# Selective scans by halves of the channels: two states with elementwise products, two with products on TensorE, per slice

## The chip, the cores and the metric

The kernel runs on one core of a Trainium2 chip. A core has a matrix engine (TensorE, PE in the profile), a vector engine (VectorE, DVE), an activation engine (ScalarE, ACT), a general engine (GpSimd, POOL) and a queue engine (SyncE, SP) that here only starts transfers. Each engine executes its own instructions in order, and engines wait for one another by semaphores. The metric is the device time of one execution in microseconds (us). The kernel before takes 34339.38 us (median of three runs, 34338.59 to 34341.42).

## The reference, cut to what matters

The program is a chain of four layers on an image of 256 x 256 positions with 128 channels. Layer 0 is an attention along rows, layer 1 a selective scan in four directions, layer 2 mixes Fourier modes, layer 3 convolves by FFT. Only layer 1 is concerned. For each of the directions `k`, with 256 inner channels `d` and 16 states `n`, it computes along the 65536 positions `t`

```
delta = softplus(dts + dt_bias)
dA    = exp(delta[t, d] * A[d, n])
h     = dA * h + (delta[t, d] * x[t, d]) * B[t, n]      # the state, one recurrence per (d, n)
y[t, d] = sum_n h[d, n] * C[t, n]
```

`B` and `C` depend on position and state and are the same for all channels. `delta * x` (called `du` in the kernel) depends on position and channel and is the same for all states. The results of the four directions are added.

## The kernel before, in words

`scan_stream` computes layer 1's recurrences. It cuts each direction into 128 chunks of `CH` = 512 positions, so there are N = 512 chunks in all, one after another. Channels lie on the 128 partitions, in two halves `dh`. In a chunk there are `NG` = 8 groups of `G` = 4 states: even groups belong to half 0, odd ones to half 1. A group goes through these steps:

- `b_product` (L769): `db = B * du` for four states, 128 x 2048 elements. B comes from DRAM, broadcast to all partitions (`load_b`, L692). Of each eight groups, those in `on_pool` (three) run on POOL, the other five on DVE, which reads `du` out of PSUM.
- `scans` (L771 to L808): two scans of 1024 elements, each two states of 512 in a row. Two exponentials on ACT (L787) write `dA` into one of two PSUM tiles `das`. At the joint of the two states `dA` has to be zero, so that the second state starts anew. The position `mid` is set to zero by a memset on DVE (L783), but only at the very first group and once more where the direction of time turns; after that no one writes `mid`. A small activation (L791) adds the second state's carried value to `db` at the joint. Then DVE scans (L802).
- `keep_state` (L813): ACT copies the last column of the four states.
- `c_product` (L817): POOL multiplies `h` by C (`load_c`, L698).
- `sums` (L827): 16 transposing matmuls of 128 x 128 with the identity add the four states up in a PSUM bank per half, `ys`.

Once per half and chunk `delta` and `du` are made: `dt` (a matmul into PSUM, L704), `soft_abs`, `soft_exp`, `soft_sum` (softplus on ACT and PE, L716 to L729), `delta_copy` (L739), `delta_x` (DVE, L747), and for one half `du_copy` (ACT, L758). `xproj` (L672) and `xd_copy` (L684) make B and C of a later chunk. `y_turn`, `y_back` and `y_out` (L824 to L880) turn the summed result back and take it out of PSUM; `y_start` (L844) begins a new sum.

The order on every engine is written out by hand: the loop at L906 calls the steps in the order in which each engine has them, under a manual schedule. The tile framework adds the semaphore waits. It derives them from the order of the calls and from the tiles that each touches, and orders two engines on one PSUM tile whichever of its elements they touch. All transfers of the stage are issued by SP, in order.

Of the kernel before, what the change touches and what calls it, by code (L numbers as in the profile page):

```python
# [576 lines left out]
def scan_stream(c, xc2, y, w):  # L577
# [8 lines left out]
    G, BL, NG = 4, 1024, 8  # L586
    R = y[1].shape[3]
    NW = BL // S
    on_pool = (2, 4, 6)
    b_order = {0: (3,), 1: (4,), 2: (5,), 3: (6, 7), 4: (8,), 6: (10,)}  # L590
# [5 lines left out]
    with ExitStack() as a:  # L596
        st = a.enter_context(tc.tile_pool(name="l1b_st", bufs=1))
        io = a.enter_context(tc.tile_pool(name="l1b_io", bufs=2))
        bcp = a.enter_context(tc.tile_pool(name="l1b_bc", bufs=3))
        wk = a.enter_context(tc.tile_pool(name="l1b_wk", bufs=2))  # L600
        dram = a.enter_context(tc.tile_pool(name="l1b_dr", bufs=4, space=DRAM))
        ps1 = a.enter_context(tc.tile_pool(name="l1b_p1", bufs=1, space=PSUM))
        states = [st.tile([P, 2, 16], F32, name=f"l1b_state{k}") for k in range(4)]

        xds = [st.tile([64, CH], F32, name=f"l1b_xd{i}") for i in range(3)]
        for s in states:
            nc.vector.memset(s, 0.0)
        for xd in xds:
            nc.vector.memset(xd[32:64], 1.0)
        ys = [ps1.tile([P, CH], F32, name=f"l1b_y{dh}") for dh in range(2)]  # L610
        das = [ps1.tile([P, 2, CH], F32, name=f"l1b_da{i}") for i in range(2)]


        mm = ps1.tile([P, CH], F32, name="l1b_mm")
        du1 = ps1.tile([P, CH], F32, name="l1b_du")
        blocks, bcs, bbs, ccs, soft, dls, dbs, hs, hcs, yts = ({} for _ in range(10))
# [49 lines left out]

        def xproj(ch):
            if ch >= N:
                return
            k = chunks[ch][0]  # L670
            for dh in range(2):
                nc.tensor.matmul(  # L672
                    du1[:40],
                    w["xproj"][:, dh, k, :],
                    in_block(blocks[ch][0], ch, dh),
                    start=dh == 0,
                    stop=dh == 1,
                )

        def xd_copy(ch):  # L680
            if ch >= N:
                return
            xd = xds[ch % 3]
            nc.scalar.copy(xd[:40], du1[:40])  # L684
            bc = bcs[ch] = dram.tile([32, CH], F32, name="l1b_bc")
            nc.sync.dma_start(bc, xd[8:40])

        def load_b(m):
            if m < 4 * N:
                n0 = m % 4 * G  # L690
                bb = bbs[m] = bcp.tile([P, G, CH], F32, name="l1b_bb")
                nc.sync.dma_start(bb, bcs[m // 4][n0 : n0 + G][None].to_broadcast([P, G, CH]))  # L692

        def load_c(m):
            if m < 4 * N:
                n0 = 16 + m % 4 * G
                cc = ccs[m] = bcp.tile([P, G, CH], F32, name="l1b_cc")
                nc.sync.dma_start(cc, bcs[m // 4][n0 : n0 + G][None].to_broadcast([P, G, CH]))  # L698


        def dt(ch, dh):
            if ch >= N:
                return
            nc.tensor.matmul(  # L704
                mm,
# [6 lines left out]
        def soft_abs(ch):  # L712
            if ch >= N:
                return
            soft[ch] = wk.tile([P, CH], F32, name="l1b_tail", bufs=1)
            nc.scalar.activation(soft[ch], mm, AF.Abs)  # L716
            nc.scalar.activation(mm, mm, AF.Relu)

        def soft_exp(ch):
            if ch >= N:  # L720
                return
            tail = soft[ch]
# [3 lines left out]
        def soft_sum(ch):  # L726
            if ch >= N:
                return
            nc.tensor.matmul(  # L729
                mm, c.ident, soft.pop(ch), start=False, stop=True, skip_group_check=True  # L730
            )

        def delta_copy(ch, dh):

            if ch >= N:
                return
            k = chunks[ch][0]
            dl = dls[ch, dh] = wk.tile([P, CH], F32, name=f"l1b_dl{dh}")
            nc.scalar.copy(dl, mm)  # L739
            af = dls[ch, dh, "first"] = wk.tile([P, 16], F32, name=f"l1b_af{dh}")  # L740
            t0 = CH - 1 if k >= 2 else 0
            nc.scalar.activation(af, w["A"][:, k, dh], AF.Exp, scale=dl[:, t0 : t0 + 1])

        def delta_x(ch, dh):
            if ch >= N:
                return
            nc.vector.tensor_tensor(  # L747
                like_block(du1 if dh else mm, ch),
                like_block(mm, ch),
                in_block(blocks[ch][0], ch, dh),  # L750
                ALU.mult,
            )

        def du_copy(ch):
            if ch >= N:
                return
            dls[ch, "du"] = wk.tile([P, CH], F32, name="l1b_dus")
            nc.scalar.copy(dls[ch, "du"], mm)  # L758

        def b_product(g):  # L760
            ch, j = divmod(g, NG)
            if ch >= N:
                return
            db = dbs[g] = wk.tile([P, G, CH], F32, name="l1b_db", bufs=5)
            if j in on_pool:
                eng, du = nc.gpsimd, dls[ch, "du"]
            else:
                eng, du = nc.vector, du1 if j % 2 else mm
            eng.tensor_tensor(db, bbs[g // 2], du[:, None, :].to_broadcast([P, G, CH]), ALU.mult)  # L769

        def scans(g, extras):  # L771
            ch, j = divmod(g, NG)
            k, dh, n0, rev = chunks[ch][0], j % 2, j // 2 * G, chunks[ch][0] >= 2
            db = dbs.pop(g).rearrange("p g t -> p (g t)")
            h = hs[g] = wk.tile([P, G, CH], F32, name="l1b_h", bufs=3)
            hf = h.rearrange("p g t -> p (g t)")
            dl, af = dls[ch, dh], dls[ch, dh, "first"]
            mid = CH - 1 if rev else CH
            for i in range(2):
                one, two = n0 + 2 * i + rev, n0 + 2 * i + 1 - rev  # L780
                da = das[i].rearrange("p g t -> p (g t)")
                if g == 0 or ch == N // 2 and j == 0:
                    nc.vector.memset(da[:, mid : mid + 1], 0.0)  # L783
                for n in (one, two):
                    o = n % 2 * CH
                    lo, hi = (0, CH) if n == one else (0, CH - 1) if rev else (1, CH)
                    nc.scalar.activation(  # L787
                        da[:, o + lo : o + hi], dl[:, lo:hi], AF.Exp, scale=w["A"][:, k, dh, n : n + 1]
                    )
                first = db[:, 2 * i * CH + mid : 2 * i * CH + mid + 1]  # L790
                nc.scalar.activation(  # L791
                    first,
                    states[k][:, dh, two : two + 1],
                    AF.Identity,
                    scale=af[:, two : two + 1],
                    bias=first,
                )
                sl = slice(2 * i * CH, 2 * i * CH + 2 * CH)
                h_, a_, d_ = hf[:, sl], da, db[:, sl]
                if rev:  # L800
                    h_, a_, d_ = h_[:, ::-1], a_[:, ::-1], d_[:, ::-1]
                nc.vector.tensor_tensor_scan(  # L802
                    h_, a_, d_, states[k][:, dh, one : one + 1], ALU.mult, ALU.add
                )
                if i == 0 and g:
                    keep_state(g - 1)
                for extra in extras[i]:
                    extra()  # L808

        def keep_state(g):  # L810
            ch, j = divmod(g, NG)
            k, dh, n0 = chunks[ch][0], j % 2, j // 2 * G
            nc.scalar.copy(states[k][:, dh, n0 : n0 + G], hs[g][:, :, 0 if k >= 2 else CH - 1])  # L813

        def c_product(g):
            hc = hcs[g] = wk.tile([P, G, CH], F32, name="l1b_hc", bufs=3)
            nc.gpsimd.tensor_tensor(hc, hs[g], ccs[g // 2], ALU.mult)  # L817
            hs.pop(g - 1, None)

        def y_turn(ch, dh):  # L820
            if ch < 0:
                return
            yt = yts[dh] = wk.tile([P, CH], F32, name="l1b_yt", bufs=1)
            nc.scalar.copy(yt, ys[dh])  # L824

        def turned(to, b, part, start, stop):
            nc.tensor.matmul(  # L827
                to[:, bass.ts(b, P)],
                part,
                c.ident,  # L830
                start=start,
                stop=stop,
                is_transpose=True,
                skip_group_check=True,
            )

        def y_start(ch, dh):
            k = chunks[ch][0]
            xc, yo = blocks[ch]
            for b in range(CH // P):  # L840
                if k == 2:
                    turned(ys[dh], b, in_block(yo, ch, dh)[:, bass.ts(b, P)], b == 0, True)
                if k == 0:
                    nc.tensor.matmul(  # L844
                        ys[dh][:, bass.ts(b, P)],
# [7 lines left out]
        def sums(g):  # L853
            ch, j = divmod(g, NG)
            new = chunks[ch][0] % 2 == 1
            if j < 2 and not new:
                y_start(ch, j)
            hc = hcs.pop(g)
            for i in range(G):
                for b in range(CH // P):  # L860
                    turned(
                        ys[j % 2], b, hc[:, i, bass.ts(b, P)], new and j < 2 and i + b == 0, True
                    )

        def y_back(ch, dh):
            if ch < 0:
                return
            add = chunks[ch][0] == 3
# [927 lines left out]
```

## Time and profile before

| what | value |
|---|---|
| median of the runs | 34339.38 us |
| the profiled execution's own time | 34336.33 us |
| its span, first to last instruction | 34334.6 us |
| DVE busy | 31153.8 us (91%) |
| POOL busy | 27466.5 us (80%) |
| PE busy | 23728.7 us (69%) |
| ACT busy | 23345.7 us (68%) |
| the scans (L802): first start, last start | 3912.9 us, 29617.4 us |
| mean granted clock of TensorE | 0.804 |

The page of a profile has a row for each group of instructions: line, engine, operation, output and inputs by the program's names, shapes, count, then busy time, the mean duration of one in ns, and the idle time of the engine just before them with what ended most of it. The stage of the scans takes three quarters of the time, so a row's share of the whole understates its share of the stage.

### The profile page before, as it was taken

How to read it: one execution, taken by the hardware profiler on the slowest of the kernel's cores; microseconds unless marked ns; L12 is line 12 of the kernel's file. 1: busy time of each engine (PE TensorE's matmuls, PEld its weight loads, DVE VectorE, ACT ScalarE, POOL GpSimd, SP SyncE). 2: the span in 40 equal slices, each digit the busy share in tenths (PEclk: the TensorE clock that was granted, in tenths of full speed). 3: DMA queues.
4: the chain of work that ended last, by engine and by line, in shares of the span. 5: the costliest groups of instructions: out<-in, count | busy, mean ns of one | idle time of the engine just before them, and what ended most of it. 6: DMA issues, size and time to landing. Idle time of an engine off the chain costs nothing. (4 is left out here: it accounts for less than half of the span.)

```text
span 34334.6 us, 330861 instructions
## 1 busy us (share of the span) xinstructions
PE 23728.7 (69%) x108660; PEld 15714.0 (46%) x108660; DVE 31153.8 (91%) x23679; ACT 23345.7 (68%) x48143; POOL 27466.5 (80%) x6996
## 2 busy tenths in 40 slices
PE   7999766666666666666666666666666666799877
PEld 3554444444444444444444444444444444434444
DVE  6668999999999999999999999999999999873699
ACT  3667777777777777777777777777777777532477
POOL 2446899999999999999999999999999999720000
PEclk9999877777777777777777777777887787899999
DMA  3113455555555555555555555555555555675111
GB/s 141 45 45 123 185 190 189 191 190 190 189 191 189 189 190 190 190 189 191 195 201 199 201 200 200 199 202 200 200 202 200 201 199 201 209 233 160 68 35 33
DMA packets 2076823, 5952.61 MB, mean 173 GB/s; under 512 B 115207, under 2 KB 1379608, under 8 KB 1499222
## 3 DMA queue, kind: packets, MB, share of 16 engines
q1 hardware_dynamic: 1939122, 5860.18, 47.2%
q10 hardware_dynamic: 135972, 71.27, 0.7%
q8 instruction: 855, 14.01, 0.2%
q14 instruction: 874, 7.16, 0.1%
HBM read 5238.41 MB, written 692.58 MB: 173 GB/s over the span
## 5 line engine op out<-in xcount | busy, mean ns | idle before, releaser
L802 DVE TENSOR_TENSOR_SCAN l1b_h<-l1b_da,l1b_state,l1b_db 128x1024 f32<-128x1024 f32 x8192 | 18847.8, 2337 | 678.8 <-ACT l1b_db L791 594.3
L817 POOL TENSOR_TENSOR l1b_hc<-l1b_h,l1b_cc 128x2048 f32<-128x2048 f32 x4096 | 18480.3, 4537 | 430.8 <-DVE l1b_h L802 430.8
L787 ACT ACTIVATE l1b_da<-l1b_dl,l_alog 128x512 f32<-128x512 f32 (+1 forms) x16384 | 11298.8, 690 | 2793.1 <-DVE l1b_h L802 2484.9
L827 PE MATMUL l1b_y<-ident,l1b_hc 128*128 128x128 f32 x65536 | 10636.3, 331 | 3479.7 <-POOL l1b_hc L817 3474.4
L827 PEld LDWEIGHTS l1b_y<-ident,l1b_hc 128*128 128x128 f32 x65536 | 9760.0, 175 | 5869.2 <-POOL l1b_hc L817 4330.6
L769 POOL TENSOR_TENSOR l1b_db<-l1b_bb,l1b_dus 128x2048 f32<-128x2048 f32 x1536 | 6965.5, 4535 | 46.6 <-DMA l1b_bb<-l1b_bc 46.6
L769 DVE TENSOR_TENSOR l1b_db<-l1b_bb,l1b_du 128x2048 f32<-128x2048 f32 x2048 | 4656.9, 2274 | 35.1
L704 PE MATMUL l1b_mm<-l1b_xd,l_dtw 41*128 41x512 f32 x2048 | 1753.9, 950 | 3303.1 <-ACT l1b_dus L758 2746.7
L791 ACT ACTIVATE l1b_db<-l1b_state,l1b_db,l1b_af 128x1 f32<-128x1 f32 x8192 | 3045.4, 372 | 0.0
L813 ACT COPY l1b_state<-l1b_h 128x4 f32<-128x4 f32 x4095 | 788.9, 193 | 2387.2 <-DVE l1b_h L802 2386.4
L729 PE MATMUL l1b_mm<-l1b_tail,ident 128*128 128x512 f32 x2048 | 1470.0, 808 | 911.4 <-ACT l1b_tail L724 908.9
L704 PEld LDWEIGHTS l1b_mm<-l1b_xd,l_dtw 41*128 41x128 f32 x2048 | 438.1, 266 | 3576.6 <-ACT l1b_dus L758 2867.5
L332 POOL TENSOR_TENSOR l0b_e<-l0b_e,l0b_den 128x1024 f32<-128x1024 f32 x512 | 969.0, 1893 | 1372.9 <-DVE l0b_den L331 726.4
L827 PE MATMUL l1b_y<-ident,l1b_yt 128*128 128x128 f32 x4096 | 877.7, 352 | 1448.2 <-ACT l1b_yt L824 1448.2
L827 PEld LDWEIGHTS l1b_y<-ident,l1b_yt 128*128 128x128 f32 x4096 | 597.2, 177 | 1890.0 <-ACT l1b_yt L824 1709.1
L758 ACT COPY l1b_dus<-l1b_mm 128x512 f32<-128x512 f32 x512 | 299.6, 585 | 1387.7 <-DVE l1b_db L769 1387.3
L769 DVE TENSOR_TENSOR l1b_db<-l1b_bb,l1b_mm 128x2048 f32<-128x2048 f32 x512 | 1171.0, 2287 | 18.2 <-ACT l1b_dus L758 0.7
L672 PE MATMUL l1b_du<-l1b_xc,l_xproj 128*40 128x512 f32 x2048 | 1158.0, 694 | 32.4 <-DMA l1b_xc<-l_xc 31.6
L308 DVE CUSTOM_DVE_ANT_0 l0b_e<-l0b_sc,l0b_bias 128x256 f32<-128x256 f32 x2048 | 745.4, 420 | 414.8 <-PE l0b_sc L297 411.4
L323 ACT ACTIVATE l0b_e<-l0b_e,l0b_top 128x256 f32<-128x256 f32 x2048 | 1012.1, 498 | 0.9 <-DVE l0b_top L308 0.9
L739 ACT COPY l1b_dl<-l1b_mm 128x512 f32<-128x512 f32 x1024 | 587.6, 574 | 520.4 <-DVE l1b_du L747 516.1
L729 PEld LDWEIGHTS l1b_mm<-l1b_tail,ident 128*128 128x128 f32 x2048 | 386.9, 237 | 1069.6 <-ACT l1b_tail L724 1065.5
(282 smaller groups left out, 30409.0 us busy)
## 6 DMA issues: line engine op xcount, KB each, us to landing
l1b_bb<-l1b_bc SPq DMA_DIRECT2D x2048, 1024.0 KB
l1b_cc<-l1b_bc SPq DMA_DIRECT2D x2048, 1024.0 KB
l1b_xc<-l_xc SPq DMA_DIRECT2D x128, 1024.0 KB
l_y<-l1b_yo SPq DMA_DIRECT2D x128, 1024.0 KB
l1b_xc<-l_xct SPq DMA_DIRECT2D x256, 512.0 KB
l_y<-l1b_yo SPq DMA_DIRECT2D x256, 512.0 KB
l_xc<-l1a_o SPq DMA_DIRECT2D x64, 1024.0 KB
l_xct<-l1a_ot SPq DMA_DIRECT2D x16, 4096.0 KB
```

The source lines that it names most:

```text
L323: nc.scalar.activation(e[:, i], e[:, i], AF.Exp, scale=-1.0, bias=top[:, i : i + 1], accum_out=den[:, i : i + 1],)
L332: nc.gpsimd.tensor_tensor(e, e, den[:, :, None].to_broadcast([P, 4, S]), ALU.mult)
L672: nc.tensor.matmul(du1[:40], w["xproj"][:, dh, k, :], in_block(blocks[ch][0], ch, dh), start=dh == 0, stop=dh == 1,)
L704: nc.tensor.matmul(mm, w["dt"][:, chunks[ch][0], dh * P : dh * P + P], xds[ch % 3][0:41], start=True, stop=True,)
L729: nc.tensor.matmul(mm, c.ident, soft.pop(ch), start=False, stop=True, skip_group_check=True)
L769: eng.tensor_tensor(db, bbs[g // 2], du[:, None, :].to_broadcast([P, G, CH]), ALU.mult)
L787: nc.scalar.activation(da[:, o + lo : o + hi], dl[:, lo:hi], AF.Exp, scale=w["A"][:, k, dh, n : n + 1])
L791: nc.scalar.activation(first, states[k][:, dh, two : two + 1], AF.Identity, scale=af[:, two : two + 1], bias=first,)
L802: nc.vector.tensor_tensor_scan(h_, a_, d_, states[k][:, dh, one : one + 1], ALU.mult, ALU.add)
L813: nc.scalar.copy(states[k][:, dh, n0 : n0 + G], hs[g][:, :, 0 if k >= 2 else CH - 1])
L817: nc.gpsimd.tensor_tensor(hc, hs[g], ccs[g // 2], ALU.mult)
L827: nc.tensor.matmul(to[:, bass.ts(b, P)], part, c.ident, start=start, stop=stop, is_transpose=True, skip_group_check=True,)
```

## The change

`scan_stream` is rewritten. A chunk's two halves of the channels now come one after the other, as units `u` (two per chunk). A unit has `NS` = 4 slices `q`, and a slice has four states: states 2q and 2q+1 with `db` from an elementwise product as before, and states 8+2q and 9+2q with `db` made by TensorE.

- `product`: `db` for states 0 to 3 on DVE and 4 to 7 on POOL, once each per unit.
- `fill`: `db` of the other two states as a matmul. `du` is transposed (`du_turn`, copied to SBUF by `dut_copy`), and multiplied by matrices `diag` that have B on the diagonal. A matmul's 256 columns are 128 positions x 2 states, so that the two states lie interleaved in a pair of PSUM banks. The diagonals are written to DRAM in pieces of 16 bytes (`b_turn`, `b_copy`) into images that are zero elsewhere, and read back whole (`load_d`, 1 MB each).
- `scan_two`: one scan of 1024 as before, `dA` in a pair of PSUM banks, the memset of `mid` now in every slice.
- `scan_each`: two scans of 512, with `dA` in SBUF and `db` in PSUM, every second element.
- Three pairs of PSUM banks are used in turns: slice g takes pair 2g mod 3 for `scan_two`'s `dA` and pair 2g+1 mod 3 for `scan_each`'s `db`.

The core of the diff (steps of softplus and of the output change only their indices, from chunk and half to unit):

```diff
-        ys = [ps1.tile([P, CH], F32, name=f"l1b_y{dh}") for dh in range(2)]
-        das = [ps1.tile([P, 2, CH], F32, name=f"l1b_da{i}") for i in range(2)]
+        pairs = [ps1.tile([P, 2 * CH], F32, name=f"l1b_pair{i}") for i in range(3)]
+        yp = ps1.tile([P, CH], F32, name="l1b_y")
+        mi = ps1.tile([P, CH], F32, name="l1b_mi")
...
+        def b_turn(ch):
...
+            for b in range(NB):
+                turned(mi[:, bass.ts(b, 40)], xds[ch % 3][0:40, bass.ts(b, P)], b == 0)
+
+        def b_copy(ch):
...
+            nc.scalar.copy(bt, v[:, :, 16:24])
+            for i in range(2):
+                f = far[i][ch % 3]
+                to = bass.AP(
+                    f.tensor, f.offset, [[NB * P * G + G, P], [P * G, NB], [1, G]]
+                )
+                nc.sync.dma_start(to, bt[:, :, i * G : i * G + G])
+
+        def load_d(ch, i):
+            if ch < N:
+                nc.sync.dma_start(diag[i], far[i][ch % 3])
...
+        def product(u, i):
...
+            eng, du = (nc.gpsimd, dus[u % 2]) if i else (nc.vector, mi)
+            eng.tensor_tensor(dbs[i], bbs[i], du[:, None, :].to_broadcast([P, G, CH]), ALU.mult)
+
+        def du_turn(u):
+            if u < 2 * N:
+                for b in range(NB):
+                    turned(mi[:, bass.ts(b, P)], dus[u % 2][:, bass.ts(b, P)], b == 0)
+
+        def dut_copy(u):
+            if u < 2 * N:
+                nc.scalar.copy(duts[u % 2].rearrange("p b m -> p (b m)"), mi)
+
+        def fill(g):
...
+            to = pairs[(2 * g + 1) % 3]
+            for b in range(NB):
+                nc.tensor.matmul(
+                    to[:, 2 * b * P : 2 * b * P + 2 * P],
+                    duts[u % 2][:, b],
+                    diag[q // 2][:, b, :, q % 2 * 2 : q % 2 * 2 + 2],
...
+        def scan_two(g):
...
+            da = pairs[2 * g % 3]
+            mid = CH - 1 if rev else CH
+            nc.vector.memset(da[:, mid : mid + 1], 0.0)
+            one, two = 2 * q + rev, 2 * q + 1 - rev
+            for n in (one, two):
...
+                nc.scalar.activation(
+                    da[:, o + lo : o + hi], dl[:, lo:hi], AF.Exp, scale=w["A"][:, k, dh, n : n + 1]
+                )
...
+            nc.vector.tensor_tensor_scan(
+                h_, a_, d_, states[k][:, dh, 2 * q + one : 2 * q + one + 1], ALU.mult, ALU.add
+            )
+
+        def scan_each(g):
...
+            da = wk.tile([P, 2, CH], F32, name="l1b_da", bufs=2)
+            db = pairs[(2 * g + 1) % 3].rearrange("p (t n) -> p t n", n=2)
+            for j in range(2):
+                n = 8 + 2 * q + j
+                nc.scalar.activation(
+                    da[:, j], dls[u], AF.Exp, scale=w["A"][:, k, dh, n : n + 1]
+                )
+                h_, a_, d_ = hs[g][:, 2 + j], da[:, j], db[:, :, j]
...
+                nc.vector.tensor_tensor_scan(
+                    h_, a_, d_, states[k][:, dh, at : at + 1], ALU.mult, ALU.add
+                )
...
+        for u in range(2 * N):
+            ch, dh = divmod(u, 2)
+            nxt = u + 1
+            for s in range(NS):
+                g = NS * u + s
+                if s == 0:
+                    dt(nxt)
+                scan_two(g)
                 if s == 1:
+                    soft_exp(nxt)
                 if s == 2:
+                    delta_copy(nxt)
+                    delta_x(nxt)
+                    y_turn(u - 1)
+                    product(nxt, 0)
+                    du_copy(nxt)
                 if s == 3:
+                    du_turn(nxt)
+                    dut_copy(nxt)
+                fill(g + 1)
+                if s == 2:
+                    y_back(u - 1)
+                if s == 3:
+                    if dh:
+                        b_turn(ch + 2)
+                    else:
+                        xproj(ch + 2)
+                scan_each(g)
                 if s == 0:
+                    soft_abs(nxt)
+                if s == 1:
+                    soft_sum(nxt)
                 if s == 2:
+                    y_out(u - 1)
+                keep_state(g - 1)
+                if s == 3:
+                    if dh:
+                        b_copy(ch + 2)
+                    else:
+                        xd_copy(ch + 2)
+                sums(g - 2)
+                if s == 3:
+                    product(nxt, 1)
                 c_product(g)
+                if dh == 0:
+                    if s < 2 and ch:
+                        load_c(ch, 2 + s)
+                    if s == 3:
+                        load_b(ch + 1, 0)
+                else:
+                    if s == 1:
+                        load_d(ch + 1, 0)
+                        load_b(ch + 1, 1)
+                    if s == 2:
+                        load_c(ch + 1, 0)
...
+                    if s == 3:
+                        load_d(ch + 1, 1)
+                        load_c(ch + 1, 1)
```

## The prediction

> **What bounds the kernel now.** I read the costliest groups first, to find the stage and its engines.
>
> ```profile
> L802 DVE TENSOR_TENSOR_SCAN l1b_h<-l1b_da,l1b_state,l1b_db 128x1024 f32<-128x1024 f32 x8192 | 18847.8, 2337 | 678.8 <-ACT l1b_db L791 594.3
> L817 POOL TENSOR_TENSOR l1b_hc<-l1b_h,l1b_cc 128x2048 f32<-128x2048 f32 x4096 | 18480.3, 4537 | 430.8 <-DVE l1b_h L802 430.8
> L769 DVE TENSOR_TENSOR l1b_db<-l1b_bb,l1b_du 128x2048 f32<-128x2048 f32 x2048 | 4656.9, 2274 | 35.1
> ```
>
> The scans run from 3912.9 us to 29617.4 + 2.3 us, so a chunk takes 25706.8 / 512 = 50.21 us. POOL has 11 products per chunk, 11 x 4.537 = 49.9 us; DVE 16 scans, 5 products and 2 multiplications for `du`, 16 x 2.337 + 5 x 2.276 + 2 x 0.673 = 50.1 us (instructions overlap a little at their ends). The busy time by stretch confirms it for one chunk (columns: length, then PE, PEld, DVE, ACT, POOL busy, TensorE clock, DMA share, GB/s; below it two short stretches):
>
> ```profile
> 10000.00:10050.21 50.21, 32.49 (x164) 24.71 (x164) 48.80 (x24) 36.14 (x76) 49.39 (x12) 0.76 0.49 190
> 10017.50:10020.00 2.50, 2.50 (x10) 1.69 (x9) 2.48 (x2) 2.07 (x5) 2.50 (x1) 0.50 0.00 0
> 10025.00:10027.50 2.50, 2.50 (x19) 1.97 (x18) 1.98 (x2) 2.47 (x6) 2.50 (x2) 1.00 0.98 385
> ```
>
> POOL and DVE are both full, and ACT, PE and the transfers have room. The waits say why DVE hardly waits for the exponentials: there are two `das`, so ACT works one scan ahead. The exception is what I looked for in the timeline: the memset of `mid`. Before, it happens four times. This is the start of the stage:
>
> ```profile
> 3911.08 0.06 DVE L783 MEMSET l1b_da<- 128x1 f32 x1
> ...
> 3911.17 1.41 ACT L787 ACTIVATE l1b_da<-l1b_dl,l_alog 128x512 f32<-128x512 f32 x2 [5.01 <-DVE l1b_da L783]
> 3912.52 0.37 ACT L791 ACTIVATE l1b_db<-l1b_state,l1b_db,l1b_af 128x1 f32<-128x1 f32 x1
> 3912.93 2.35 DVE L802 TENSOR_TENSOR_SCAN l1b_h<-l1b_da,l1b_state,l1b_db 128x1024 f32<-128x1024 f32 x1 [1.79 <-ACT l1b_db L791]
> 3915.29 0.06 DVE L783 MEMSET l1b_da<- 128x1 f32 x1
> ...
> 3917.14 2.35 DVE L802 TENSOR_TENSOR_SCAN l1b_h<-l1b_da,l1b_state,l1b_db 128x1024 f32<-128x1024 f32 x1 [1.79 <-ACT l1b_db L791]
> ```
>
> The exponentials wait for the memset although they write other elements, and DVE, which issues the memset right before the scan, then stands for 1.79 us: two exponentials, the small activation, two handovers.
>
> **What the Trainium skill says.** "PSUM — Partial Sum Buffer", section "PSUM bank collisions raise a hardware error": accesses by two engines have to be kept apart by bank, not by address. The trace agrees with such an ordering: `du_copy` only reads a bank that DVE's product also only reads, and waits for it:
>
> ```profile
> ACT l1b_dus L758 <- DVE l1b_db L769: 54.3, 20, 2.7
> ```
>
> "DVE: opcode table, instruction layouts, handler registers and perf-mode slots", section 6, "Datapath and trigger behaviour": the scan runs at half throughput. L802 agrees: 2337 ns for 1024 elements, where a product takes 2274 ns for 2048. "TensorE: Matmul & The Clock Gate", Part 1: after idle windows the clock is halved, after sustained work full. The two short stretches above show 0.50 and 1.00.
>
> **The change part by part.** All per unit (half a chunk), of four slices.
>
> *POOL.* Four C-products and one B-product, 5 x 4.537 = 22.7 us; a chunk 45.4 instead of 49.9.
>
> *DVE's own work.* A scan of 512 has no row. From 2337 ns, of which at most some 200 are fixed (a product's 2274 against 673 for a quarter of the length gives (4 x 673 - 2274) / 3 = 139): half is 1.17, plus half the fixed part, 1.27. `db` is read at every second element of PSUM; the bounds are 1.17 (no fixed part) and 2.34 (a full price per skipped element). I take 1.27, since a scan leaves a read twice a product's time. A slice: 2.34 + 2 x 1.27 + memset 0.06 = 4.94. A unit: 4 x 4.94 + product 2.28 + `delta_x` 0.67 = 22.7. Alone, this would be a gain too.
>
> *The memset in every slice.* In the calls, the memset of slice g+1 stands after `scan_each` of slice g on DVE, and the built kernel has the first exponential of `scan_two` wait for exactly that memset. With three pairs, the pair itself has been free since `scan_each` of slice g-1, but ACT may not use the time. Behind the waiting exponential on ACT stand the second one and the small activation, and DVE's scan waits for those: the 1.79 us shown above, now in each slice. 4 x 1.79 = 7.2 us per unit. Nothing covers it: DVE has nothing between memset and scan. Less 0.06 for each of the scans that overlap the one before (four in a row take 9.31, not 9.35; two 4.58, not 4.67), a slice is about 6.6, four 26.4.
>
> *`du_copy` after `product`.* In the third slice DVE does `scan_two`, `delta_x`, `product`, then `scan_each`. `du_copy` reads the same bank as the product, waits for its end as L758 does now, and the exponentials of `scan_each` stand behind it on ACT: 0.585 + 0.69 + 0.1 of handover = 1.35 us in which DVE waits.
>
> Sum: 26.4 + 2.28 + 0.67 + 1.35 = 30.7 per unit, 61.4 per chunk.
>
> *PE.* Added are four fills (each four f32 matmuls of 256 columns) and `du_turn`. Prices at full clock from rows of now: four matmuls of 128 columns (L844) 1.06 us, so a fill 1.9; four transposes 0.5 (L827 x16 takes 1.91); two matmuls of `xproj` about 1.8; all double at half clock (x16 takes 3.67). The moving operand of a fill is strided; bounds are 1.9 and 3.8. I take 1.9. Two chains decide:
> 1. In the third slice `y_out` stands on ACT behind the exponentials. After it PE does `y_start` (1.06, only in the first direction), `sums` 1.91, `du_turn` 0.5; then ACT `dut_copy` 0.58 and one exponential 0.69; with handovers 5.0 us, half clock 8.2. DVE needs that exponential about 5.5 us after `y_out`'s end (6.66 from one `scan_each` to the next, less the 1.2 in which ACT gets to `y_out`'s end). Hidden at full clock, 2.7 late per unit at half.
> 2. After the last `scan_two`, PE does the fill, then `xproj` (first half) or `b_turn` (second); ACT copies that out (`xd_copy` 0.56), and the next slice's exponentials stand behind. First half: 1.9 + 1.8 + 0.56 + 0.2 = 4.4, against 2.5 of `scan_each`: 1.9 late; at half clock 5.5. Second half: 0.2 late; at half clock 2.5.
>
> A chunk is 61.4 + 1.9 + 0.2 = 63.5 at full clock, and 61.4 + 5.4 + 5.5 + 2.5 = 74.8 at half. Before, the mean is 0.76, half of the time at half clock; but chain 2 follows straight on dense PE work, and PE gets more to do. I take a fifth of the difference: 65.8.
>
> *ACT.* Eight small activations fewer per chunk (8 x 0.372), one more `du_copy`, two `dut_copy` (0.58 each), one small `b_copy`: -1.0 us, with room in any case (36 of 50 now).
>
> *Transfers.* Per chunk 8 MB as before: 2 of B, 4 of C, 2 of diagonals, plus two stores of 512 pieces of 16 bytes. "DMA: Bandwidth & Descriptors", "Specifications", gives 512 bytes as the least for full rate. Queue q10's packets (0.5 KB in the mean) took 28 ns of an engine, q1's (3 KB) 134 ns: 1024 such over 16 engines are 1.8 to 8.6 us. On SP they stand ahead of `load_d(ch+1, 1)`, which PE needs in the second slice of the next unit, about 9 us later; 1 MB takes 2.6 at the 410 GB/s seen, and I allow 2 until it is seen. Covered at the lower price (6.4 us), 4 late for PE at the upper, and most of that within PE's slack of a slice. I take nothing.
>
> *Around.* Zeroing and storing the diagonals once is 6 MB, under 30 us.
>
> Total: (65.8 - 50.21) x 512 = 7980; 34336 + 7980 = 42300 us. The profiled execution is 3 us from the median, which doesn't matter here.
>
> **The rivals.**
> - *Faster: the exponentials aren't held.* If the memset's wait cost nothing, POOL (45.4) would bound again with about 0.4 of coupling: 512 x -4.4 = -2260, 32080 us. For it: ACT and PE are far from full. Against it: the four cases in the trace. It decides when the wait per slice falls under (50.2 - 45.4) / 8 = 0.6 us.
> - *PE becomes the bound.* Half clock throughout: 74.8 per chunk, 46900 us. For it: at 0.50 its work doubles. Against it: the clock rises with work.
> - *The small stores or strided operands are dear.* Stores at twice the upper price, or fills at 3.8: about 5 us more per chunk, 44900 us.
>
> **How the numbers follow.** My forecast's case has 0.8, PE as the bound 0.08, dear stores or strides 0.08, faster 0.03, and 0.01 for no change. A difference of 0.2% (69 us) is about what can be told from none. Range: low is 62.4 per chunk (shorter fixed parts, full clock), 40600; the upper end takes in the dear stores and half of the way to half clock, 45500.
>
> **What would show it.** Per step: the scan of 1024 waits for the small activation 4096 times, 7300 us in sum; the scan of 512 waits for its exponential at least 1024 times, some 1400 us; scans of 512 last 1.27 us; POOL is at 69% of the stage instead of 98%, DVE near 69%; the clock is 0.8 or more. Wrong would be: exponentials that start during `scan_each`, a 512-scan over 1.5 us, or PE waits on diagonals.

## The result, and the profile after

The changed kernel takes 42081.1 us (median of four runs, 42074.9 to 42092.4), the kernel before in the same job 34339.0. The ratio is 1.2255, with an interval of 1.2234 to 1.2277: 7742 us more. The span of the profiled execution is 42081.9 us. The scans run from 3917.5 us to 37374.0 + 1.3 us, so a chunk takes 33457.8 / 512 = 65.35 us instead of 50.21; 15.14 x 512 = 7750 us is the whole loss. The stages around the scans are unchanged.

The costliest groups of the kernel after, from its page (busy time, mean of one in ns, and after the second bar the idle time before them and what ended it):

```profile
L895 POOL TENSOR_TENSOR l1b_hc<-l1b_h,l1b_cc 128x2048 f32<-128x2048 f32 x4096 | 18529.0, 4524 | 10378.2 <-DVE l1b_pair L840 8980.1
L860 DVE TENSOR_TENSOR_SCAN l1b_h<-l1b_pair,l1b_state,l1b_db 128x1024 f32<-128x1024 f32 x4096 | 9624.1, 2350 | 9363.4 <-ACT l1b_db L850 9363.4
...
L879 DVE TENSOR_TENSOR_SCAN l1b_h<-l1b_da,l1b_state,l1b_pair 128x512 f32<-128x512 f32 x8192 | 9972.8, 1259 | 1478.7 <-ACT l1b_da L872 1280.9
...
L845 ACT ACTIVATE l1b_pair<-l1b_dl,l_alog 128x512 f32<-128x512 f32 (+1 forms) x8192 | 5667.4, 692 | 6539.9 <-DVE l1b_pair L840 6406.5
...
L799 ACT COPY l1b_dus<-l1b_mi 128x512 f32<-128x512 f32 x1024 | 600.2, 586 | 3903.9 <-DVE l1b_db L805 3903.5
```

Before, the idle column of the scans and of POOL's products held a few hundred microseconds. Now DVE stands for 9363 us ahead of the scan of 1024 and for 1479 us ahead of the scans of 512, together 10842 us; POOL stands for 10378 us, and the name beside it is the memset (L840), which is the last thing that DVE does before it stands. The exponentials (L845) wait for that same memset. So DVE waits for ACT, and ACT waits for DVE.

The busy time by stretch (length, then PE, PEld, DVE, ACT, POOL busy, TensorE clock, DMA share, GB/s) for 2000 us inside the stage:

```profile
10000.00:12000.00 2000.00, 1452.76 (x7410) 1120.04 (x7408) 1359.20 (x1111) 1075.46 (x2162) 1391.35 (x309) 0.89 0.43 147
```

DVE is busy for 68% and POOL for 70%, where both were near 98%. No engine is full any more: the stage is bound by handovers. How they follow one another is seen in the timeline of the kernel after, DVE alone, over one unit (start, duration, line, and in brackets the idle time before and what ended it):

```profile
10010.96 0.06 DVE L840 MEMSET l1b_pair<- 128x1 f32 x1
10013.06 2.35 DVE L860 TENSOR_TENSOR_SCAN l1b_h<-l1b_pair,l1b_state,l1b_db 128x1024 f32<-128x1024 f32 x1 [2.05 <-ACT l1b_db L850]
10015.33 2.43 DVE L879 TENSOR_TENSOR_SCAN l1b_h<-l1b_da,l1b_state,l1b_pair 128x512 f32<-128x512 f32 x2
10017.76 0.06 DVE L840 MEMSET l1b_pair<- 128x1 f32 x1
10019.67 2.35 DVE L860 TENSOR_TENSOR_SCAN l1b_h<-l1b_pair,l1b_state,l1b_db 128x1024 f32<-128x1024 f32 x1 [1.85 <-ACT l1b_db L850]
...
10026.27 2.35 DVE L860 TENSOR_TENSOR_SCAN l1b_h<-l1b_pair,l1b_state,l1b_db 128x1024 f32<-128x1024 f32 x1 [1.85 <-ACT l1b_db L850]
10028.54 0.67 DVE L793 TENSOR_TENSOR l1b_mi<-l1b_mi,l1b_xc 128x512 f32<-128x512 f32 x1
10029.25 2.29 DVE L805 TENSOR_TENSOR l1b_db<-l1b_bb,l1b_mi 128x2048 f32<-128x2048 f32 x1
10032.81 2.45 DVE L879 TENSOR_TENSOR_SCAN l1b_h<-l1b_da,l1b_state,l1b_pair 128x512 f32<-128x512 f32 x2 [1.27 <-ACT l1b_da L872]
```

The same 1.85 us stands behind the memsets (here 2.05 in the unit's first slice), and 1.27 us ahead of the scans of 512 in the third slice, after the product. What ACT does in the 1.85 us is in the full timeline of the kernel after, in another unit; the last three lines are the first slice of the unit that follows:

```profile
12003.66 0.06 DVE L840 MEMSET l1b_pair<- 128x1 f32 x1
...
12003.75 1.42 ACT L845 ACTIVATE l1b_pair<-l1b_dl,l_alog 128x512 f32<-128x512 f32 x2 [2.39 <-DVE l1b_pair L840]
...
12005.10 0.37 ACT L850 ACTIVATE l1b_db<-l1b_state,l1b_db,l1b_af 128x1 f32<-128x1 f32 x1
...
12005.56 2.35 DVE L860 TENSOR_TENSOR_SCAN l1b_h<-l1b_pair,l1b_state,l1b_db 128x1024 f32<-128x1024 f32 x1 [1.85 <-ACT l1b_db L850]
...
12022.81 0.19 ACT L718 COPY l1b_bt<-l1b_mi 128x32 f32<-128x32 f32 x1 [4.32 <-PE l1b_mi L676]
12022.89 1.42 ACT L845 ACTIVATE l1b_pair<-l1b_dl,l_alog 128x512 f32<-128x512 f32 x2
...
12024.71 2.35 DVE L860 TENSOR_TENSOR_SCAN l1b_h<-l1b_pair,l1b_state,l1b_db 128x1024 f32<-128x1024 f32 x1 [3.48 <-ACT l1b_db L850]
```

Ahead of the exponentials at 12003.75 ACT has been idle for 2.39 us, longer than the two of them take (1.42 us); it starts them 0.03 us after the memset has ended. At 12022.81 it is not the memset that is last: ACT is held in `b_copy` by PE for 4.32 us, and the scan stands for 3.48 us.

If each of the 4096 slices has 1.85 us of the first kind, that is 7578 us; the remaining 9363 - 7578 = 1785 us are the second kind, in the first slice of a unit. The trace bears this out slice by slice: the 1024 first slices wait 3.59 us in the mean (1.85 to 6.74), the 3072 others 1.85 us in the mean.

### The profile page after: what moved, and what is told of

It is laid out like the page before. It is cut to its first block, busy times and chain, and to the rows that moved or that the text cites. A ratio compares the mean times of both kernels' runs of the same rounds, so it can differ in the third digit from the quotient of the medians.

```text
span 42081.9 us, 420657 instructions
## 1 busy us (share of the span) xinstructions
PE 31418.3 (75%) x147572; PEld 21813.3 (52%) x147572; DVE 28727.8 (68%) x30333; ACT 22641.9 (54%) x46095; POOL 25251.7 (60%) x6484
## 4 chain that ended last, share of the span: by engine, by line
DVE 32%; ACT 28%; PE 20%; issue 11%; DMA 1%; DVEq 0%; POOL 0%; SPq 0%; ACTq 0%; POOLq 0%
DVE l1b_h L879 15%; ACT l1b_pair L845 12%; PE l1b_pair L823 7%; ACT l1b_da L872 6%; DVE l1b_h L860 5%; DVE l1b_db L805 5%; PE l1b_y L676 3%; ACT l1b_db L850 3%; PE l1b_mi L691 2%; DVE l1b_mi L793 1%; DVE l1a_mm L522 1%; PE l1b_mi L676 1%; PE l2f_fp L1466 1%; PE l2f_op L1473 1%; ACT l1b_tail L760 1%
## 5 line engine op out<-in xcount | busy, mean ns | idle before, releaser
L860 DVE TENSOR_TENSOR_SCAN l1b_h<-l1b_pair,l1b_state,l1b_db 128x1024 f32<-128x1024 f32 x4096 | 9624.1, 2350 | 9363.4 <-ACT l1b_db L850 9363.4
L823 PE MATMUL l1b_pair<-l1b_diag,l1b_dut 128*128 128x256 f32 x32768 | 10436.3, 470 | 7449.4 <-DVE l1b_h L860 5808.2
L823 PEld LDWEIGHTS l1b_pair<-l1b_diag,l1b_dut 128*128 128x128 f32 x32768 | 7076.6, 227 | 10385.7 <-DVE l1b_h L860 6702.4
L879 DVE TENSOR_TENSOR_SCAN l1b_h<-l1b_da,l1b_state,l1b_pair 128x512 f32<-128x512 f32 x8192 | 9972.8, 1259 | 1478.7 <-ACT l1b_da L872 1280.9
L676 PE MATMUL l1b_y<-ident,l1b_hc 128*128 128x128 f32 x65536 | 8830.2, 293 | 953.9 <-ACT l1b_state L889 948.3
L676 PEld LDWEIGHTS l1b_y<-ident,l1b_hc 128*128 128x128 f32 x65536 | 8207.3, 153 | 2306.9 <-issue 2067.3
L845 ACT ACTIVATE l1b_pair<-l1b_dl,l_alog 128x512 f32<-128x512 f32 (+1 forms) x8192 | 5667.4, 692 | 6539.9 <-DVE l1b_pair L840 6406.5
L872 ACT ACTIVATE l1b_da<-l1b_dl,l_alog 128x512 f32<-128x512 f32 x8192 | 5431.4, 711 | 0.0
L805 POOL TENSOR_TENSOR l1b_db<-l1b_bb,l1b_dus 128x2048 f32<-128x2048 f32 x1024 | 4644.4, 4536 | 65.8 <-DMA l1b_cc<-l1b_bc 65.7
L805 DVE TENSOR_TENSOR l1b_db<-l1b_bb,l1b_mi 128x2048 f32<-128x2048 f32 x1024 | 2341.9, 2287 | 50.4 <-DMA l1b_bb<-l1b_bc 15.3
L850 ACT ACTIVATE l1b_db<-l1b_state,l1b_db,l1b_af 128x1 f32<-128x1 f32 x4096 | 1521.8, 372 | 0.0
```

The lines of the kernel that those rows point to most:

```text
L676: nc.tensor.matmul(to, part, c.ident[0 : part.shape[0], 0 : part.shape[0]], start=start, stop=True, is_transpose=True, skip_group_check=True,)
L805: eng.tensor_tensor(dbs[i], bbs[i], du[:, None, :].to_broadcast([P, G, CH]), ALU.mult)
L823: nc.tensor.matmul(to[:, 2 * b * P : 2 * b * P + 2 * P], duts[u % 2][:, b], diag[q // 2][:, b, :, q % 2 * 2 : q % 2 * 2 + 2], start=True, ...
L845: nc.scalar.activation(da[:, o + lo : o + hi], dl[:, lo:hi], AF.Exp, scale=w["A"][:, k, dh, n : n + 1])
L850: nc.scalar.activation(first, states[k][:, dh, 2 * q + two : 2 * q + two + 1], AF.Identity, scale=af[:, two : two + 1], bias=first,)
L860: nc.vector.tensor_tensor_scan(h_, a_, d_, states[k][:, dh, 2 * q + one : 2 * q + one + 1], ALU.mult, ALU.add)
```

## The experiments

Three theories stand in the expectations. **M** is that of the prediction: the memset in every slice makes the exponentials of ACT wait, and two smaller holds on ACT (`du_copy` behind the product, `xd_copy` and `b_copy` behind PE) add to it. **P**: PE, with the added fills, sets the pace, and ACT's and DVE's waits only show it. **S**: the small stores, the diagonals' loads or the strided operands are dear.

### The memset a slice earlier

```diff
+        def clear(g):
+            u, q = divmod(g, NS)
+            if u < 2 * N:
+                mid = CH - 1 if chunks[u // 2][0] >= 2 else CH
+                nc.vector.memset(pairs[2 * g % 3][:, mid : mid + 1], 0.0)
...
         def scan_two(g):
...
-            nc.vector.memset(da[:, mid : mid + 1], 0.0)
...
+        clear(0)
...
+                clear(g + 1)
                 scan_two(g)
```

The same memsets, in the same number; each now goes a slice ahead, between `scan_each` of one slice and `scan_two` of the next, to the pair that is free by then.

> The changed kernel with one thing moved: the memset of the joint for slice g+1 is called before scan_two of slice g instead of right before scan_two of slice g+1. Its wait then ends with scan_each of slice g-1, a whole slice ahead. Theory M (the exponentials are held by the memset): the 1.85 us before each scan of 1024 goes, 8 x 1.85 = 14.8 us of 65.35 per chunk; but a slice shrinks to 4.75 us, so the two chains over PE lose cover (at full clock about 1.4 late twice, 3.8 once, 2.2 once), and 56 to 58 us per chunk remain: 37300 to 38300 us. The idle time of DVE before the scan of 1024 falls from 9363 us to under 4000, and what remains stands in the first slice of a unit. Theory P (PE with its fills sets the pace): no change beyond 1%, 41700 to 42500. Theory S (stores and reloads of the diagonals): no change either.

Measured: 36751.4 us, ratio 1.0700 (1.0682 to 1.0718). The groups of this kernel in the list by line:

```profile
L865 DVE TENSOR_TENSOR_SCAN l1b_h<-l1b_pair,l1b_state,l1b_db 128x1024 f32<-128x1024 f32 x4096 | 9624.6, 2350 | 2882.8 <-ACT l1b_db L855 2835.4 <-POOL l1b_db L805 39.3 <-issue 5.0
L884 DVE TENSOR_TENSOR_SCAN l1b_h<-l1b_da,l1b_state,l1b_pair 128x512 f32<-128x512 f32 x8192 | 9985.9, 1261 | 2212.6 <-ACT l1b_da L877 2212.6
L850 ACT ACTIVATE l1b_pair<-l1b_dl,l_alog 128x512 f32<-128x512 f32 (+1 forms) x8192 | 5663.3, 691 | 133.5
```

The exponentials' wait for the memset is gone (6540 to 134 us of idle), and 5330 of the 7742 us are back, from the place of one instruction of 0.06 us. P and S, which expected nothing, fall as the main cause: PE has the same work, the transfers too. But 7578 us stood there to be won, and 2248 of them are missing; the expected range began at 37300 us, so more came back than expected. Other waits grew as this one went: 1479 to 2213 us ahead of the scans of 512, and 1785 to 2835 us ahead of the scan of 1024, together 1784 us. By slice, it is not `du_copy` that grew: ahead of the third slice's scans of 512 there are 1303 us in both kernels. What grew is the wait ahead of the fourth slice's scans of 512, 176 to 910 us, and the one ahead of the first slice's scan of 1024, 1783 us beyond the memset's share to 2574: the places of the prediction's two chains over PE, which DVE's standing seems to have hidden in part. Most of the remaining 464 us lies on DVE too: it is idle for 305 us ahead of the memsets instead of 31, and for 151 us ahead of `delta_x` instead of almost none.

### No fills

```diff
                     dut_copy(nxt)
-                fill(g + 1)
```

This kernel leaves out the products of B and `du` for half of the states; everything else is as after.

> The changed kernel without the fills: the scans of 512 read what the PSUM pair holds, all else stays. Theory M: only the fill's 1.9 us in the chain to xd_copy and b_copy goes, 1.5 to 3 us per chunk: 40500 to 41300. Theory P: PE loses 8 x 2.1 us of work per chunk and the time falls by most of it, under 36000.

Measured: 40435.0 us, ratio 1.1775 (1.1752 to 1.1799). From the list of what waits for what, in the view of `h` (idle time in us, times):

```profile
  ACT l1b_db L850: 7581.5, 4095
...
  ACT l1b_da L872: 1586.7, 1316
```

PE has 6700 us less to do (24682 us busy instead of 31418), and the kernel gets only 1646 us faster, a little more than expected (40500 at least). P had it under 36000. What went is the second kind of wait: ahead of the scans of 1024, 4095 waits remain and 7581.5 / 4095 = 1.851 us each, with nothing over. (Those of the scans of 512 grew by 0.1 us per unit.) So the fill stands at the head of the hold of `xd_copy` and `b_copy`, as the prediction's chain 2 had it, and the work of the fills as such is not what the kernel after waits for.

### The memset in every scan of the kernel before

```diff
-                if g == 0 or ch == N // 2 and j == 0:
-                    nc.vector.memset(da[:, mid : mid + 1], 0.0)
+                nc.vector.memset(da[:, mid : mid + 1], 0.0)
```

> The kernel before with one thing added: the memset of the joint ahead of every scan, 16 per chunk. PE and the transfers stay as they were. Theory M: each scan waits 1.79 us after a memset of 0.06, 16 x 1.85 = 29.6 us more per chunk, less what DVE stood idle anyway (1.4): 78 to 80 per chunk, 48500 to 49700 us. Theory P: nothing beyond the memsets' own 16 x 0.06 us per chunk, 34340 to 34900.

Measured: 49716.2 us, ratio 1.4478 (1.4449 to 1.4507). Its timeline:

```profile
12000.13 0.06 DVE L782 MEMSET l1b_da<- 128x1 f32 x1
12000.22 1.42 ACT L786 ACTIVATE l1b_da<-l1b_dl,l_alog 128x512 f32<-128x512 f32 x2 [2.45 <-DVE l1b_da L782]
...
12001.58 0.37 ACT L790 ACTIVATE l1b_db<-l1b_state,l1b_db,l1b_af 128x1 f32<-128x1 f32 x1
...
12001.98 2.35 DVE L801 TENSOR_TENSOR_SCAN l1b_h<-l1b_da,l1b_state,l1b_db 128x1024 f32<-128x1024 f32 x1 [1.79 <-ACT l1b_db L790]
```

Ahead of the 8192 scans DVE now stands for 14906 us (9230 put down to the small activation, 5677 to `keep_state`, which comes right after it on ACT), 1.82 us each. This is the hold alone, without fills, stores, strides or a change of layout. The time lies 16 us above the expected range. A chunk has 16 scans and gets (49716 - 34339) / 512 = 30.0 us longer, 1.88 for each scan: the wait of 1.82, the memset of 0.06, and the overlap of scans that follow one another, which is lost and which the expectation left out, less the little that DVE had waited before. The two `das` in turn don't help, since DVE issues the memset only when it is about to scan.

### The two other holds, each alone

The exponentials of `scan_each` ahead of `du_copy` in the third slice (`each_exps` is the first half of `scan_each`, cut off):

```diff
                     product(nxt, 0)
+                    each_exps(g)
                     du_copy(nxt)
...
+                if s != 2:
+                    each_exps(g)
                 scan_each(g)
```

> The changed kernel with only the exponentials of scan_each moved ahead of du_copy in the third slice. The scans of 512 waited 1479 us in sum, 1.44 us per unit. That goes: 40500 to 40800 us if nothing comes in its place; up to 41400 if the later du_copy delays du_turn and with it the last slice.

Measured: 40766.3 us, ratio 1.1870 (1.1846 to 1.1894), 1315 us under the kernel after. The scans of 512 in the list by line of this kernel:

```profile
L888 DVE TENSOR_TENSOR_SCAN l1b_h<-l1b_da,l1b_state,l1b_pair 128x512 f32<-128x512 f32 x8192 | 9963.0, 1258 | 136.3 <-ACT l1b_da L873 136.3
```

Of their 1479 us of waiting, 136 are left; the third slice's 1303 us are gone altogether.

`xd_copy` and `b_copy` behind the exponentials of the next unit's first `scan_two`:

```diff
+                scan_two(g)
+                if s == 0 and u:
+                    if dh:
+                        xd_copy(ch + 2)
+                    else:
+                        b_copy(ch + 1)
                 if s == 0:
                     dt(nxt)
-                scan_two(g)
...
-                if s == 3:
-                    if dh:
-                        b_copy(ch + 2)
-                    else:
-                        xd_copy(ch + 2)
```

> The changed kernel with only the copies xd_copy and b_copy moved behind the next unit's exponentials; the memset stays in its place. The scans of 1024 waited 9363 us in sum, 7578 of it at least for the memset (4096 x 1.85); the other 1786 us are chain 2. 1000 to 1800 us less, 40300 to 41100 us. Theory P: no change.

Measured: 40432.4 us, ratio 1.1773 (1.1749 to 1.1796), 1649 us under the kernel after, of the 1785 that were put down to this hold. It is the time of the kernel without fills, within 3 us: moving the copies wins as much as leaving the fills out. The scans of 1024 in this kernel's list by line wait for 7680 us in all, the memset's share and little more:

```profile
L860 DVE TENSOR_TENSOR_SCAN l1b_h<-l1b_pair,l1b_state,l1b_db 128x1024 f32<-128x1024 f32 x4096 | 9624.8, 2350 | 7679.5 <-ACT l1b_db L850 7033.8 <-ACT l1b_bt L718 627.2 <-POOL l1b_db L805 18.5
```

### The mends together

First the early memset with the early exponentials:

> As memset_early, and the exponentials of scan_each stand ahead of du_copy on ACT in every third slice. Theory M with my second term: the 1.44 us that the first scan of 512 waits per unit (2.9 per chunk) go, and du_copy's end doesn't move: 51 to 54 us per chunk, 34800 to 36300 us. If the time stays at that of memset_early, the wait was only moved.

Measured: 35048.7 us, ratio 1.0207 (1.0186 to 1.0227). The wait of the scans of 512 for their exponentials fell to 127 us; a new one came up, 1277 us ahead of the scan of 1024 for POOL's B-product (349 times). Its cause stays open; it is absent from the next run's list.

Then all three:

> As early_du, and xd_copy and b_copy stand behind the exponentials of the next unit's first scan_two on ACT (with dt behind them on PE). Theory M with my chain 2 (the copies that wait for PE hold the next slice's exponentials): in early_du a chunk takes 51.6 us; the wait at the start of each unit goes but for what the exponentials of scan_each then wait behind the copies, some 0.5 us per unit: 2 to 4 us less per chunk, 48 to 50 us, 33200 to 34300 us. If chain 2 is only a name for a wait that something else causes, within 0.5% of early_du's 35049.

Measured: 33779.4 us (33779.2 to 33780.2), ratio 0.9836 (0.9821 to 0.9850). That is 1.6% faster than the kernel before. The three mends alone bring 5330, 1315 and 1649 us, 8294 together; all three in one kernel bring 8302. That the sums agree so well is in part chance: in the order taken here the second mend brings 1703 us and the third 1269. In the list of waits of this kernel:

```profile
DVE l1b_h L865 <- ACT l1b_db L855: 2001.5, 2046, 3.4
DVE l1b_h L893 <- ACT l1b_da L878: 310.6, 637, 2.1
```

The scan of 1024 still waits in half of the slices, and 1541 us of this stand in the second slice of a unit, right after the copies that were moved: ACT starts its exponentials only when everything of the slice before is off its queue.

### ACT one scan ahead

The last edit puts the exponentials of the next `scan_two` right behind those of `scan_each`, ahead of all copies, and `du_turn` and `dut_copy` ahead of `sums`, a slice earlier (`two_exps` is the first half of `scan_two`, cut off):

```diff
                 scan_two(g)
                 if s == 2:
+                    delta_copy(nxt)
+                    delta_x(nxt)
+                    y_turn(u - 1)
+                    product(nxt, 0)
+                each_exps(g)
+                two_exps(g + 1)
...
                 if s == 2:
-                    delta_copy(nxt)
-                    delta_x(nxt)
-                    y_turn(u - 1)
-                    product(nxt, 0)
-                    each_exps(g)
                     du_copy(nxt)
-                if s == 3:
-                    du_turn(nxt)
-                    dut_copy(nxt)
                 fill(g + 1)
                 if s == 2:
                     y_back(u - 1)
+                    du_turn(nxt)
...
                     y_out(u - 1)
+                    dut_copy(nxt)
                 keep_state(g - 1)
```

> All of the above, and ACT works one scan ahead: the exponentials and the small activation of the next slice's scan of 1024 are issued right behind those of scan_each, ahead of the copies, and du_turn and dut_copy come a slice earlier, ahead of the sums. If the wait chains over ACT are all that held the changed plan, it is now bound by its own sums, POOL 45.4 us and DVE about 45 per chunk: 45.5 to 47.5 per chunk, 31900 to 33000 us, faster than the kernel before (34339). If PE with the fills is the next bound (about 44 us of work per chunk at full clock), 48 to 51: 33200 to 34700.

Measured: 31720.9 us (31710.9 to 31735.4), ratio 0.9238 (0.9222 to 0.9253): 2618 us faster than the kernel before, 10360 faster than the kernel after, and 179 under the range expected for it. The edit moves several steps at once, and no run parts them. Its list by line, and its busy time by stretch:

```profile
L919 POOL TENSOR_TENSOR l1b_hc<-l1b_h,l1b_cc 128x2048 f32<-128x2048 f32 x4096 | 19185.1, 5208 | 4.8 <-DVE l1b_h L903 4.6 <-DVE l1b_pair L836 0.2
...
L875 DVE TENSOR_TENSOR_SCAN l1b_h<-l1b_pair,l1b_state,l1b_db 128x1024 f32<-128x1024 f32 x4096 | 9624.5, 2350 | 369.1 <-POOL l1b_hc L919 356.4 <-issue 9.1 <-ACT l1b_db L856 3.4
```

```profile
5000.00:25000.00 20000.00, 17601.71 (x102383) 13328.62 (x102382) 19386.10 (x15972) 15320.45 (x31053) 19999.79 (x4437) 1.00 0.70 218
```

POOL is busy for 19999.8 of 20000 us, and what DVE still waits for ahead of the scan of 1024 is POOL, so POOL's ten products per chunk are the bound now, with DVE close behind at 97%: the scans run from 3917.6 to 26997.9 us, 45.08 us per chunk, 4.51 for each product. (The mean of 5208 ns in the first line isn't slower work. POOL's busy time in all is 25253 us, against 25252 in the kernel after; in this trace a record on POOL begins 0.8 us in the mean before the one ahead of it ends, which counts that time twice.) DVE's waits for ACT ahead of the scans have shrunk to a few microseconds. PE is busy for 88% at full clock, and doesn't bind either. The idea of the change, less work for POOL, is thus worth what it seems to be worth, once ACT isn't held.

## Why the prediction was right, step by step

The forecast was 42300 us with 65.8 us per chunk; it came to 42081 and 65.35. By the prediction's steps, in us per chunk:

| step | predicted | measured |
|---|---|---|
| DVE's own work, less overlaps | 44.4 | 67.4% of 65.35 = 44.1 |
| memset in every slice | 8 x 1.79 = 14.3 | 8 x 1.85 = 14.8 |
| `du_copy` behind the product | 2 x 1.35 = 2.7 | 1303 / 512 = 2.5 (third slices) |
| chain 1 (`y_out` to `dut_copy`) | a fifth of 5.4 = 1.1 | 176 / 512 = 0.3 (fourth slices) |
| chain 2 (fill to `xd_copy`, `b_copy`) | 2.1 + a fifth of 5.9 = 3.3 | 1785 / 512 = 3.5 |
| sum | 65.8 | 65.2 |

The measured column splits DVE's busy and idle time by slice, so that its sum comes to the length of a chunk by itself; the single rows are what confirms the prediction.

- **The memset.** It makes 14.8 of the 21.2 us per chunk (10842 / 512) that DVE waits ahead of its scans. The step could be read off four places in the kernel before, and its price off the timeline there. Taking the memset out of the way in the kernel after and putting it in the way in the kernel before show it from both sides. The prediction also named why the third pair doesn't help.
- **The scans of 512.** 1259 ns in the mean, for a chosen 1270; 2350 ns for the long one. Reading every second element of PSUM costs little if anything: with no price for it, 1259 and 2350 ns leave 2 x 1259 - 2350 = 168 ns of fixed part, between the 139 that the products gave and the 200 that the forecast allowed. No run reads the same `db` without the stride.
- **The `du_copy` wait.** 1.27 us in the timeline, 1.35 forecast (its three terms add up to 1.375), and gone when the exponentials were put ahead.
- **The two chains.** Chain 2 is right in its place (only in a unit's first slice, gone without fills, gone with the copies moved). Its sum is right in part by luck. With the fifth taken, the forecast has 2.6 us late per chunk behind `xproj` and `xd_copy` and 0.7 behind `b_turn` and `b_copy`; by slice, the kernel after has 2.2 and 1.3, and the two errors cancel. Chain 1 was oversized. Its sum takes in `y_start` for every chunk, though the prediction itself says that those matmuls run only in the first direction. There, in a quarter of the chunks, 149 of the 176 us stand, 1.2 us per chunk, about as forecast; in the other three directions it is under 0.1.
- **The clock.** A fifth of the way to half clock was picked, not derived. The stage's clock of 0.89 is (1 - 0.89) / 0.5, about a fifth of the way from 1.00 to 0.50, so the mean was met, but not evenly. The fills' matmuls last 388 ns in the median and 797 at most. Over 550 ns last 28% of all of them, but 13% in the fills ahead of `xproj` and 66% in those ahead of `b_turn`. That fits the two halves of chain 2: the first was less late than forecast, the second more.
- **POOL.** 70% busy, 69% forecast; DVE 68%.
- **The rivals.** *PE as the bound* falls with the run without fills, and again with the last kernel, which has all of PE's matmuls and takes 31721 us. *Dear stores or strides* fall too: the list of waits of the kernel after has

```profile
PE l1b_pair L823 <- DMA l1b_diag<-l1b_far: 115.8, 37, 3.9
```

37 waits for a diagonal in the whole run, 0.2 us per chunk. A fill takes 2.08 us at full clock in the timeline, against 1.9 estimated. *Faster* (32080 us) was not what the change did, but with all the holds gone and ACT ahead the kernel came to 31721. The memset's wait alone, on which that rival rested, was not enough: 36751.

The forecast of 42300 us was met within 0.5%, and the mechanism that carries most of it was shown. Of the runs after it, four ended outside the expected range: the early memset (36751, range from 37300), the kernel without fills (40435, from 40500), ACT ahead (31721, from 31900), each faster than expected, and the memset in the kernel before (49716, range up to 49700). In the first of these I had expected the chains over PE to come out dearer: at least 2800 of the 7578 us were to stay lost, and 2248 did.

## What to carry to other kernels

In these kernels a write of one element of a tile held ACT off all the others: each memset of 0.06 us cost a wait of 1.85 us. Where the consumer clears a corner of a buffer that a producer fills, under an order kept by whole tiles, issue the clear when the buffer comes free, not when it is next used, or the buffers in turn are worth one buffer only. When no engine of a stage is full (in the stretch shown above none was over 73%), look for two engines that wait for each other in turn (here "DVE waits for ACT L850" beside "ACT waits for DVE L840"), and read from the timeline which instruction sits late on its queue. Mend all such holds before judging the idea behind a change: each mend alone left this kernel slower than before, the three together made it 1.6% faster, and with ACT a scan ahead it was 7.6% faster.

## What I had not expected

- The TensorE clock rose as the waits went, though PE's work stayed the same: 0.89 in the stretch from 10000 to 12000 us of the kernel after, 0.91 with the early memset, 1.00 with all three mends and with ACT ahead. PE's busy time fell with it, from 31418 to 29653, 28049 and 27908 us. The kernel before, with less work for PE, had 0.74 there. PE's steps in the chains got shorter with it: the fills' matmuls last 470 ns in the mean in the kernel after, 424 with the early memset, 400 with all three mends. How much of the gains came from this is open, since no run parts it from the rest.
- Without fills the clock went the other way, to 0.73 in that stretch, although the kernel was shorter.
